# A layered attention and expert network: the initial loads in order of use, and the doubled context copied on chip

## The chip, the cores and the metric

The kernel runs as one program on one core of a Trainium2 chip. The metric is device time in microseconds (us), from one launch to its end; lower is better. The core has five engines with a queue each: PE multiplies matrices, ACT (ScalarE) and DVE (VectorE) and POOL (GpSimd) do elementwise work, SP (SyncE) issues transfers. ACT and POOL can issue transfers too. All queues are served in order: an instruction that waits holds back everything behind it on its engine.

## What is computed

Four layers, each a cross attention from the tokens to a small context followed by a feed-forward part, over 4 sequences of 512 tokens with 256 features; the context has 64 rows for each sequence. All in float32. Only the first two lines matter here:

```python
x = x + _L0_xattn_ref(_layernorm(x), ctx_1024, Wq, bq, Wkv, bkv, Wo, bo)
x = x + _L0_ffn_ref(_layernorm(x), router_w, gate_proj, up_proj, down_proj)
...

def _L0_xattn_ref(layer_input, cross_attn_input, Wq, bq, Wkv, bkv, Wo, bo):
    q = layer_input @ Wq + bq
    kv = cross_attn_input @ Wkv + bkv
    k, v = jnp.split(kv, 2, axis=-1)
    q, k, v = map(split_heads, (q, k, v))          # 16 heads of 16
    scores = jnp.einsum('bhqd,bhkd->bhqk', q, k) * D ** (-0.5)
    weights = jax.nn.softmax(scores, axis=-1)
    out = jnp.einsum('bhqk,bhkd->bhqd', weights, v)
    return merge_heads(out) @ Wo + bo
```

`_L0_ffn_ref` sends each token to the two best of eight experts.

## The kernel before

**Tiles.** The 2048 tokens lie in 16 tiles `x0` to `x15` of 128 tokens by 256 features; four tiles make one group, and one group is one sequence. The attention of layer 0 goes over the groups 0 to 3, and the work of one group is interleaved with the rest of the one before it. When a group's attention is done, its router picks experts, and POOL scatters the tokens into a DRAM buffer `xs` with eight indirect DMAs (L827). The expert blocks then read `xs` in expert order. Since blocks are padded, `xs` has to be cleared first: `clear_regions` (L298 on) writes zeros to all of it, 16 transfers of 1040 KB (L306) and one of 130 KB (L307), from a small tile `z`.

**The start.** The constructor of `Net` issues the loads that layer 0 needs and a few that come much later, in the order in which they are written:

- SP: `x0` to `x3` (L209), then `Wkv`, `Wq`, `Wo` (`load_xattn`, all on SP, through L266), then `x4` to `x15` (L221); after them `clear_regions`, which `run` calls before the attention.
- ACT: `consts` (identity, masks, index tables), the transposed context in four pieces (L215), `vecs` (bias columns), `rows` (bias rows, spread over all partitions, 771.5 KB), `router_w`, `fw`, `ctx`, `W_router`, `Wg`; then `pairs` (helper matrices of the attention), and further on `fcT` and a second `pairs` for layer 1.

`ctxT2` holds the transposed context twice, `[128, 2, 4, 2, 64]`: for each sequence its 64 context columns stand two times side by side, so that one 128-column block can be loaded into PE to make the values of both heads of a pair. It is filled by four loads, `n` over the two halves of the features and `k` over the two copies; each writes runs of 64 numbers.

**The order of work.** In the attention PE keeps the order that the code writes; on the other engines a scheduler places each instruction. For group 0 the order on PE is: keys (`ps_k`, L399, from `Wkv` and `ctxT2`), transposes of the normalized tokens (`ps_xT`, L357), queries (`ps_q`, L478), values (`ps_v`, L436), scores (`ps_cs`, L506). The other engines in between:

- DVE takes statistics of each `x` tile (L317, L318), and makes the scale and shift of a group's layer norm (`ln_rs` L322, `ln_sh` L323) after ACT's square root (`ln_sd` L320).
- ACT normalizes the four tiles (`xn`, L325), evacuates keys (`kT`, L407) and queries (`q`, L481) with their biases from `vecs`, and copies half of each transposed group (`xnT`, L288); DVE copies the other half (L290), and masks the keys by head (`kbd`, L379).
- POOL adds the output bias to the `x` tiles (L608).

**Completion semaphores.** Each transfer from SP or ACT signals its landing on one of eight semaphores, handed out in turn over both queues. A transfer waits, on the engine that issues it, until the one that used its semaphore before, as a rule eight transfers earlier, has landed.

Of the kernel before, what the change touches and what calls it, by code (L numbers as in the profile page):

```python
# [11 lines left out]
F32 = mybir.dt.float32  # L12
# [10 lines left out]
P = 128  # L23
B, S, E = 4, 512, 256
SC = 64
NH, HD = 16, 16
NT = B * S // P
GT = S // P
NC = E // P
# [14 lines left out]
V_BQ, V_BK, V_FMB, V_BQ3, V_BK3, V_LN1, V_LN2, V_END = 0, 2, 4, 5, 7, 9, 11, 13  # L44
# [4 lines left out]
R_BV, R_BO, R_FMB, R_FCB, R_BV3, R_BO3, R_RB = range(7)  # L49
# [129 lines left out]
class Banks:  # L179


    def __init__(self, pool, tag):
        self.pool, self.tag = pool, tag
# [5 lines left out]
class Net:  # L189
    def __init__(self, ctx, tc, d, out):  # L190
        self.tc, self.nc, self.d, self.out = tc, tc.nc, d, out
        nc = self.nc

        def pool(name, bufs, **kw):
            return ctx.enter_context(tc.tile_pool(name=name, bufs=bufs, **kw))

        self.const = pool("const", 1)
        self.small = pool("small", 2)
        self.routes = pool("routes", 1)
        self.xnp = pool("xn", 2)  # L200
        self.xnTp = pool("xnT", 2)
        self.dram = pool("dram", 1, space=DRAM)
        self.flip = 0

        c = self.const
        self.x = [c.tile([P, E], F32, tag=f"x{t}", name=f"x{t}") for t in range(NT)]
        xs = d["x"].rearrange("(t p) e -> p t e", p=P)
        for t in range(GT):
            nc.sync.dma_start(self.x[t], xs[:, t])  # L209
        self.cst = self.load("consts", [P, C_END], nc.scalar)  # L210

        self.ctxT2 = c.tile([P, NC, B, 2, SC], F32, tag="ctxT2", name="ctxT2")
        for n in range(NC):
            for k in range(2):
                nc.scalar.dma_start(self.ctxT2[:, n, :, k], d["ctxT"][n * P : (n + 1) * P])  # L215
        self.vecs = self.load("vecs", [P, V_END], nc.scalar)
        n_rows = d["rows"].shape[0]
        self.rows = self.load("rows", [P, n_rows], nc.scalar, d["rows"].partition_broadcast(P))
        self.W0 = self.load_xattn("Wq", "Wkv", "Wo")
        for t in range(GT, NT):  # L220
            nc.sync.dma_start(self.x[t], xs[:, t])  # L221
        self.rw0 = self.load_w("router_w", 8, nc.scalar)
        self.fw = self.load("fw", [P, P], nc.scalar)
        self.ctx = self.load("ctx", [SC, B, E], nc.scalar, d["ctx"].rearrange("b s e -> s b e"))
        self.rw1 = self.load_w("W_router", 7, nc.scalar)
        self.rw3 = self.load_w("Wg", 8, nc.scalar)

        self.ident = self.cst[:, C_ID : C_ID + P]
        self.eps = c.tile([P, 1], F32, tag="eps", name="eps")
        nc.vector.memset(self.eps, 1e-5)  # L230
        self.nfmb = c.tile([P, 1], F32, tag="nfmb", name="nfmb")
        nc.vector.tensor_scalar(self.nfmb, self.vec(V_FMB), -1.0, None, ALU.mult)

        self.xs = self.dram.tile([8 * CAP + P, R_END], F32, tag="xs", name="xs")
        self.ys = self.dram.tile([3 * STAMP, E], F32, tag="ys", name="ys")

        self.w2q = self.dram.tile([P, W2_END], F32, tag="w2q", name="w2q")
# [32 lines left out]
        rows = self.d[name].shape[0]  # L270
        return self.load(name, [P, rows // P, n], eng, self.d[name].rearrange("(c p) n -> p c n", p=P), tag, pool)

    def load_xattn(self, q, kv, o):

        eng = self.nc.sync
        return self.load_w(kv, 2 * E, eng, "Wkv"), self.load_w(q, E, eng, "Wq"), self.load_w(o, E, eng, "Wo")

    def vec(self, i):
        return self.vecs[:, i : i + 1]
# [491 lines left out]
class Routed:  # L771
# [30 lines left out]
    def add(self, g, rows, oh1, oh2):  # L802
# [5 lines left out]
        for i in range(1, GT):  # L808
            nc.vector.tensor_tensor(pm[:, i], pm[:, i - 1], mk[:, i - 1], ALU.add)
        run = self.keep(f"run{g}", [P, n])  # L810
        nc.vector.tensor_tensor(run, pm[:, GT - 1], mk[:, GT - 1], ALU.add)
        self.run = run
        ps = net.acc.tile([P, GT, n], F32, tag="acc", name="ps_rank")
# [222 lines left out]
class Layers(Net):  # L1036
# [566 lines left out]
                last = hq  # L1603
            down(NT - 1, last)

    def xattn_linear(self, Wkv, Wq, Wo, bq, bk, bv, bo, after):
        self.xattn(
            self.query_linear(Wq, bq),
            lambda pool, b: self.values_linear(pool, b, Wkv, bv),
            HD**-0.5,  # L1610
            HD,
            Wo,
            bo,
            after=after,
            keys=lambda pool: self.keys_linear(pool, Wkv, bk),
        )

    def run(self):
        nc, d = self.nc, self.d

        def banks():
            return self.banks(mm=4, tr=2, acc=2)

        W1, W3 = [], []
        moe = Routed(self, 8, 704, d["e0gu"], d["e0d"], "e0", 2 * STAMP)
        with self.room("l0w", 1) as keep:
            self.clear_regions(keep)
            self.xattn_linear(*self.W0, V_BQ, V_BK, R_BV, R_BO, after=lambda g: self.route(moe, g, self.rw0))
        with self.room("l1k", 1, side="right") as kept:
            with self.room("l0b", side="right") as pool, banks():  # L1630

                def later():
                    yield
                    yield
                    W3.extend(self.load_xattn("w_qT", "w_kvT", "w_oT"))
                    W1.append(self.load_w("fcT", E, nc.scalar, pool=kept))
                    yield from self.ctx_ready(kept, self.keys_features)
                    yield from self.l2_weights(pool)

                with self.in_order(DVE, SP):  # L1640
                    moe.blocks(pool, later())
            self.xattn(
                self.query_features, self.values_features, 1.0 / 16.0, 2 * HD, W1[0], R_FCB, before=moe
            )
        moe = self.l1_ffn()
        with banks():
            self.l2(moe)
        moe = Routed(self, 8, 512, d["e3gu"], d["e3d"], "e3", 0)
        self.xattn_linear(*W3, V_BQ3, V_BK3, R_BV3, R_BO3, after=lambda g: self.route(moe, g, self.rw3))
        with self.room("l3b", side="right") as pool, banks():  # L1650
            with self.in_order(DVE, SP):
                moe.blocks(pool)
            out = self.out.rearrange("(t p) e -> p t e", p=P)
            with self.in_order(SP, ACT, DVE, POOL):
                queues = (nc.sync, nc.scalar)
                for t in range(NT):
                    moe.load(pool, t, queues[t % 2])
                for t in range(NT):
                    moe.take(t, nc.gpsimd if t % 3 == 2 else nc.vector)
                    queues[t % 2].dma_start(out[:, t], self.x[t])  # L1660
# [21 lines left out]
```

## Time and profile before

| | |
|---|---|
| three runs | 2026.68, 2027.1, 2034.26 us; median 2027.1 |
| the profiled execution | 2033.3 us, of which 2031.5 us is its span, from the first to the last instruction |
| PE busy over the span | 1716.2 us (84%) |
| DVE, ACT, POOL busy | 974.0 us (48%), 668.2 us (33%), 420.3 us (21%) |
| PE busy from 0 to 20 us | 3.79 us |
| ACT busy from 0 to 20 us | 1.07 us |
| the 16 DMA engines from 0 to 20 us | busy 90%, 260 GB/s |
| the 16 DMA engines from 20 to 40 us | busy 106% (of a nominal rate), 316 GB/s |
| first indirect scatter into `xs` | 106.8 us |

A line of the timeline gives start, duration, engine, source line, operation, what is written from what, and a count; in brackets, how long the engine had been idle and what ended that. A "q" after the engine's name marks its queue: the instruction issues a transfer, and the engine isn't busy. The waits view adds such idle times up. The windows view gives for each stretch of time the busy time of PE, weight loads, DVE, ACT and POOL, then the granted clock of PE, the busy share of the DMA engines, and the GB/s that they moved.

### The profile page before, as it was taken

How to read it: one execution, taken by the hardware profiler on the slowest of the kernel's cores; microseconds unless marked ns; L12 is line 12 of the kernel's file. 1: busy time of each engine (PE TensorE's matmuls, PEld its weight loads, DVE VectorE, ACT ScalarE, POOL GpSimd, SP SyncE). 2: the span in 40 equal slices, each digit the busy share in tenths (PEclk: the TensorE clock that was granted, in tenths of full speed). 3: DMA queues.
4: the chain of work that ended last, by engine and by line, in shares of the span. 5: the costliest groups of instructions: out<-in, count | busy, mean ns of one | idle time of the engine just before them, and what ended most of it. 6: DMA issues, size and time to landing. Idle time of an engine off the chain costs nothing.

```text
span 2031.5 us, 25639 instructions
## 1 busy us (share of the span) xinstructions
PE 1716.2 (84%) x8740; PEld 975.9 (48%) x8740; DVE 974.0 (48%) x2778; ACT 668.2 (33%) x1254; POOL 420.3 (21%) x590
## 2 busy tenths in 40 slices
PE   4874999999959978899999878994998887599994
PEld 2443666666624533344443344443665443355662
DVE  3644344444445333445454435446899564333333
ACT  3341322222243341335344522223445333122221
POOL 1033011111150010222222322224113112311112
PEclk8986999999979987999999989996899898699997
DMA  9613878787420000000000018772000001598895
GB/s 290 182 43 127 343 292 285 283 292 279 157 93 1 17 23 0 1 1 17 6 3 20 19 34 283 263 270 88 1 0 1 12 4 40 181 313 296 305 316 170
DMA packets 111042, 271.85 MB, mean 134 GB/s; under 512 B 15488, under 2 KB 73024, under 8 KB 100800
## 3 DMA queue, kind: packets, MB, share of 16 engines
q1 hardware_dynamic: 81728, 227.35, 33.0%
q0 software_dynamic: 10176, 28.00, 3.6%
q10 hardware_dynamic: 19008, 14.86, 2.3%
q8 instruction: 70, 1.15, 0.2%
q14 instruction: 60, 0.49, 0.1%
HBM read 220.75 MB, written 49.42 MB: 133 GB/s over the span
## 4 chain that ended last, share of the span: by engine, by line
PE 63%; DVE 14%; ACT 5%; issue 3%; POOL 3%; DMA 2%; SPq 0%; ACTq 0%; DVEq 0%; POOLq 0%
PE ps_gu L938 20%; PE ps_de L980 9%; PE ps_ms L1127 4%; PE ps_mo L1165 3%; DVE mq L1132 2%; PE ps_he L967 2%; PE ps_p L592 2%; PE ps_mx L1142 2%; PE ps_f L1549 2%; POOL xs L827 2%; PE ps_bc L571 1%; PE ps_ms L1130 1%; PE ps_xT L357 1%; PE ps_xe L924 1%; PE ps_cy L577 1%
## 5 line engine op out<-in xcount | busy, mean ns | idle before, releaser
L938 PE MATMUL ps_gu<-e_wgu,e_xT 128*128 128x352 f32 (+1 forms) x1088 | 417.8, 524 | 4.7 <-DVE e_xT L930 0.8
L938 PEld LDWEIGHTS ps_gu<-e_wgu,e_xT 128*128 128x128 f32 x1088 | 197.2, 191 | 143.9 <-issue 74.0
L980 PE MATMUL ps_de<-e_wd,e_hT 128*128 128x256 f32 x932 | 232.3, 385 | 3.8 <-ACT e_hT L288 1.5
L955 DVE TENSOR_TENSOR e_h<-e_s,ps_gu 128x352 f32<-128x352 f32 (+2 forms) x155 | 83.5, 538 | 295.5 <-PE ps_gu L938 226.9
L983 POOL DMA_INDIRECT ys<-e_y,e_to x116 | 112.4, 969 | 522.4 <-ACT e_y L982 399.5
L980 PEld LDWEIGHTS ps_de<-e_wd,e_hT 128*128 128x128 f32 x932 | 172.1, 189 | 79.5 <-issue 42.3
L954 ACT ACTIVATE e_s<-ps_gu 128x352 f32<-128x352 f32 (+2 forms) x155 | 74.0, 477 | 327.6 <-PE ps_gu L938 323.5
L1132 DVE TENSOR_REDUCE mq<-ps_ms 128x2 f32<-128x256 f32 (+3 forms) x128 | 105.7, 825 | 137.8 <-PE ps_ms L1130 136.5
L982 ACT ACTIVATE e_y<-ps_de,e_wt 128x256 f32<-128x256 f32 x116 | 54.9, 473 | 259.4 <-PE ps_de L980 248.1
L1144 ACT ACTIVATE mpr<-ps_mx 128x1024 f32<-128x1024 f32 (+3 forms) x128 | 90.0, 703 | 138.7 <-PE ps_mx L1142 135.5
L1127 PE MATMUL ps_ms<-mkT,mqT 32*128 32x512 f32 (+3 forms) x512 | 111.1, 512 | 22.7 <-DVE mq L1132 21.6
L827 POOL DMA_INDIRECT xs<-xn,e_at x96 | 93.9, 978 | 135.3 <-DVE ln_rs L322 75.7
L1142 PE MATMUL ps_mx<-mqm,mkT 32*128 32x128 f32 (+3 forms) x512 | 105.6, 489 | 1.1 <-ACT mpr L1144 1.1
L1146 POOL TENSOR_SCALAR_AFFINE_SELECT mpr<-mpr 128x256 f32<-128x256 f32 x128 | 51.8, 407 | 238.6 <-ACT mpr L1144 238.5
L1165 PE MATMUL ps_mo<-mpr,va 128*32 128x128 f32 (+3 forms) x512 | 96.4, 457 | 3.0 <-POOL mpr L1146 3.0
L357 PE MATMUL ps_xT<-consts_sb,xn 128*128 128x128 f32 x256 | 52.4, 340 | 50.9 <-ACT xn L325 36.1
L967 PE MATMUL ps_he<-consts_sb,e_h 128*128 128x128 f32 x466 | 76.2, 278 | 11.9 <-DVE e_h L955 7.9
L1549 PE MATMUL ps_f<-w,xqT 128*128 128x352 f32 x256 | 84.7, 472 | 1.2 <-ACT xqT L1540 1.2
L924 PE MATMUL ps_xe<-consts_sb,e_x 128*128 128x128 f32 x232 | 51.4, 292 | 36.6 <-DMA e_x<-xs 33.6
L927 DVE COPY e_xT<-ps_xe 128x256 f32<-128x256 f32 x78 | 33.0, 423 | 98.4 <-PE ps_xe L924 98.4
L537 PE MATMUL ps_cx<-q,kbd 32*128 32x512 f32 x256 | 45.0, 803 | 39.5 <-ACT cpr L543 39.5
L1127 PEld LDWEIGHTS ps_ms<-mkT,mqT 32*128 32x128 f32 x512 | 40.8, 195 | 77.6 <-DVE mq L1132 54.4
(314 smaller groups left out, 2769.0 us busy)
## 6 DMA issues: line engine op xcount, KB each, us to landing
e_wgu<-in_e0gu SPq DMA_DIRECT2D x39, 1408.0 KB, 6.1
e_wgu<-in_e3gu SPq DMA_DIRECT2D x39, 1024.0 KB, 5.4
e_wd<-in_e0d SPq DMA_DIRECT2D x39, 768.0 KB, 5.6
e_wd<-in_e3d SPq DMA_DIRECT2D x39, 512.0 KB, 5.6
e_wgu<-in_e1gu SPq DMA_DIRECT2D x38, 512.0 KB, 4.0
xs<-z SPq DMA_DIRECT2D x16, 1040.0 KB, 15.4
e_x<-xs SPq DMA_DIRECT2D x116, 130.0 KB, 4.9
e_wd<-in_e1d SPq DMA_DIRECT2D x38, 256.0 KB, 4.1
```

What stands on the lines that cost most here:

```text
L827: r = nc.gpsimd.indirect_dma_start(out=net.xs, out_offset=bass.IndirectOffsetOnAxis(ap=at[:, k, i : i + 1], axis=0), in_=rows[:, i], in_of ...
L938: nc.tensor.matmul(ps[:, :n], xT[:, c], wgu[:, c, cols], start=(c == 0), stop=(c == NC - 1))
L955: nc.vector.tensor_tensor(h[:, k * H : (k + 1) * H], s, u, ALU.mult)
L967: self.nc.tensor.transpose(ps[:r, f - f0], h[:, f * P : f * P + r], net.ident)
L980: nc.tensor.matmul(po[:, :E], hT[:r, f], wd[:r, f], start=(f == 0), stop=(f == self.nf - 1))
L983: r = nc.gpsimd.indirect_dma_start(out=net.ys, out_offset=bass.IndirectOffsetOnAxis(ap=at, axis=0), in_=y, in_offset=None)
L1127: nc.tensor.matmul(ps[:, r, :n], st.qT[o][rows, diag], st.kT[o][rows, :n], start=True, stop=False)
L1132: nc.vector.tensor_reduce(st.q[:, i, at : at + 2, HD], ps[:, :, :n], AX.X, ALU.max, negate=True)
L1142: nc.tensor.matmul(ps[:, r, :n], st.kT[o][rows, keys], st.qm[o][rows, j * P :], start=True, stop=True)
L1144: nc.scalar.activation(pr[:, :, :n], ps[:, :, :n], AF.Exp, scale=HD**-0.5)
L1165: nc.tensor.matmul(st.po[32 * n : 32 * n + 32, j * P :], st.va[:, j, at : at + 32], pr[:, r, : S - j * P], start=(j == 0), stop=(j == GT - 1),
L1549: nc.tensor.matmul(ps[:, :H], xT[:, c], w[:, c, k * H : (k + 1) * H], start=(c == 0), stop=(c == NC - 1))
```

## The change

It changes which queue issues each initial load and in what order, and how the second copy of the context is made:

- ACT issues five loads: `consts`, the transposed context once (one load of 256 KB into a tile of the `xnT` pool, rows of 256 numbers), `Wkv`, `vecs`, and then, as before, `pairs`.
- SP issues `x0` to `x3`, `Wq`, `Wo`, the first 512 columns of `rows`, `x4` to `x7`, `router_w` between `x7` and `x8`, the other `x` tiles, the rest of `rows`, `fw`, `ctx`, `W_router`, `Wg`, and the zeros last.
- `ctxT2` is filled by four POOL copies of 128x256 from the loaded tile, first both halves of copy 0, then those of copy 1.
- `clear_regions` is called through a new argument `then`, after the keys of layer 0 are written down, instead of before the attention.

```diff
+        ctxT = self.xnTp.tile([P, NC, S], F32, tag="xnT", name="ctxT")[:, :, : B * SC]
+        nc.scalar.dma_start(ctxT, d["ctxT"].rearrange("(c p) b s -> p c (b s)", p=P))
+        Wkv, Wq, Wo = self.load_xattn("Wq", "Wkv", "Wo", (nc.scalar, nc.sync, nc.sync))
+        self.W0 = Wkv, Wq, Wo
+        self.vecs = self.load("vecs", [P, V_END], nc.scalar)
+
+        self.rows = c.tile([P, d["rows"].shape[0]], F32, tag="rows", name="rows_sb")
+
+        def rows(part):
+            nc.sync.dma_start(self.rows[:, part], d["rows"].partition_broadcast(P)[:, part])
+
+        rows(slice(0, 2 * E))
+        for t in range(GT, NT):
+            if t == 2 * GT:
+                self.rw0 = self.load_w("router_w", 8, nc.sync)
+            nc.sync.dma_start(self.x[t], xs[:, t])
+        rows(slice(2 * E, None))
+        self.fw = self.load("fw", [P, P], nc.sync)
+        self.ctx = self.load("ctx", [SC, B, E], nc.sync, d["ctx"].rearrange("b s e -> s b e"))
+        self.rw1 = self.load_w("W_router", 7, nc.sync)
+        self.rw3 = self.load_w("Wg", 8, nc.sync)
 
         self.ctxT2 = c.tile([P, NC, B, 2, SC], F32, tag="ctxT2", name="ctxT2")
-        for n in range(NC):
-            for k in range(2):
-                nc.scalar.dma_start(self.ctxT2[:, n, :, k], d["ctxT"][n * P : (n + 1) * P])
-        self.vecs = self.load("vecs", [P, V_END], nc.scalar)
-        n_rows = d["rows"].shape[0]
-        self.rows = self.load("rows", [P, n_rows], nc.scalar, d["rows"].partition_broadcast(P))
-        self.W0 = self.load_xattn("Wq", "Wkv", "Wo")
-        for t in range(GT, NT):
-            nc.sync.dma_start(self.x[t], xs[:, t])
-        self.rw0 = self.load_w("router_w", 8, nc.scalar)
-        self.fw = self.load("fw", [P, P], nc.scalar)
-        self.ctx = self.load("ctx", [SC, B, E], nc.scalar, d["ctx"].rearrange("b s e -> s b e"))
-        self.rw1 = self.load_w("W_router", 7, nc.scalar)
-        self.rw3 = self.load_w("Wg", 8, nc.scalar)
+        for k in range(2):
+            for n in range(NC):
+                nc.gpsimd.tensor_copy(
+                    self.ctxT2[:, n, :, k], ctxT[:, n].rearrange("p (b s) -> p b s", s=SC)
+                )
...
-    def load_xattn(self, q, kv, o):
-
-        eng = self.nc.sync
-        return self.load_w(kv, 2 * E, eng, "Wkv"), self.load_w(q, E, eng, "Wq"), self.load_w(o, E, eng, "Wo")
+    def load_xattn(self, q, kv, o, queues=None):
+
+        names = ((kv, 2 * E, "Wkv"), (q, E, "Wq"), (o, E, "Wo"))
+        return [
+            self.load_w(n, w, eng, tag) for (n, w, tag), eng in zip(names, queues or 3 * [self.nc.sync])
+        ]
...
+        def keys(pool):
+            yield from self.keys_linear(pool, Wkv, bk)
+            then()
...
-            self.clear_regions(keep)
-            self.xattn_linear(*self.W0, V_BQ, V_BK, R_BV, R_BO, after=lambda g: self.route(moe, g, self.rw0))
+            self.xattn_linear(
+                *self.W0, V_BQ, V_BK, R_BV, R_BO,
+                after=lambda g: self.route(moe, g, self.rw0), then=lambda: self.clear_regions(keep),
+            )
```

**The built program.** The scheduler places the instructions anew. Compared engine by engine, PE has the same instructions in the same order in both programs. On ACT, DVE and POOL the order differs only up to the first `ps_cs` of group 0; from there on it is the same, and each instruction waits for the same others. The placements at the start that the steps below use are these:

- ACT: the five loads, a table load, `ln_sd` of group 0, the load of `fcT`, the four `xn` of group 0, the first `kT`, `ln_sd` of group 1, the second load of `pairs`, the second `kT`, the copy of `xnT`, the four `xn` of group 1, the first `q`, `ln_sd` of group 2, one `xn`, the second `q`. The table load in front of `kT` is gone.
- DVE: statistics of `x0` to `x3`, `nfmb` (from `vecs`), statistics of `x4`, `ln_rs` of group 0, statistics of `x5`, `ln_sh` of group 0, statistics of `x6` to `x11`, two `kbd`, `ln_rs` and `ln_sh` of group 1, the copy of `xnT`, two `kbd`.
- POOL: the memsets, `none`, the four copies of the context, then the additions of the bias.
- Semaphores: the loads of `vecs`, `pairs` and `fcT` wait for the landings of `x0`, the context and the first part of `rows`; `x4` and `x5` for those of `x2` and `x3`; `x9` for that of the first `pairs`; the second `pairs` for that of `x9`.

More of the change, by code (lines that the diff above doesn't have):

```diff
@@ L1604, in l2, with xattn_linear @@
             down(NT - 1, last)
-    def xattn_linear(self, Wkv, Wq, Wo, bq, bk, bv, bo, after):
+    def xattn_linear(self, Wkv, Wq, Wo, bq, bk, bv, bo, after, then=lambda: None):
+        def keys(pool):
+            yield from self.keys_linear(pool, Wkv, bk)
+            then()
         self.xattn(
@@ L1614, in xattn_linear @@
             after=after,
-            keys=lambda pool: self.keys_linear(pool, Wkv, bk),
+            keys=keys,
         )
```

## The prediction

> **What bounds the kernel now.** I read the page first: PE is busy 84% of the span, but slice by slice it starts with 4 tenths, while the DMA line starts with 9. The start is a stage of its own. Then the timeline of each engine over the first 40 us. ACT's:
>
> ```profile
> 1.25 4.00 ACTq L215 DMA_DIRECT2D ctxT<-in_ctxT  x4
> ...
> 13.55 0.67 ACTq L266 DMA_DIRECT2D ctx_sb<-in_ctx  x1
> ...
> 18.49 0.35 ACTq L266 DMA_DIRECT2D pairs_sb<-in_pairs  x1
> 18.93 1.28 ACT L407 ACT_TABLE_LOAD   x1 [18.93 <-DMA x<-in_x]
> 20.23 0.47 ACT L407 ACTIVATE kT<-ps_k,vecs_sb 128x256 f32<-128x256 f32 x1
> ...
> 21.08 1.28 ACT L320 ACT_TABLE_LOAD   x1
> 22.38 0.49 ACT L320 ACTIVATE ln_sd<-ln_mv,eps 128x4 f32<-128x4 f32 x2
> 23.16 2.57 ACT L325 ACTIVATE xn<-x,ln_sh,ln_rs 128x256 f32<-128x256 f32 x5 [0.29 <-DVE ln_sh L323]
> ```
>
> ACT computes nothing before 18.93 us. The "DMA" behind it is no operand: ACT stands behind its own 13 issues, several of them held until an older transfer lands. Next PE and DVE:
>
> ```profile
> 8.51 3.79 PE L399 MATMUL ps_k<-ctxT,Wkv_sb 128*128 128x256 f32 x8 [8.51 <-DMA Wkv_sb<-in_Wkv]
> 23.81 2.81 PE L357 MATMUL ps_xT<-consts_sb,xn 128*128 128x128 f32 x8 [11.51 <-ACT xn L325]
> 26.44 5.63 PE L478 MATMUL ps_q<-xnT,Wq_sb 128*128 128x512 f32 x8
> ...
> 32.87 1.17 PE L506 MATMUL ps_cs<-kbd,q 32*128 32x128 f32 x32
> ...
> 6.89 0.18 DVE L318 BATCH_NORM_AGGREGATE ln_mv<-ln_st 128x2 f32<-128x6 f32 x1
> ...
> 13.56 0.43 DVE L317 BATCH_NORM_STATS2 ln_st<-x 128x6 f32<-128x256 f32 x1 [2.85 <-DMA x<-in_x]
> ```
>
> Group 0's statistics are ready at 7.07 us and the keys are multiplied by 12.3, yet PE waits 11.51 us for `xn`. That hole is the prize. The waits view between 0 and 60 us says the same, and the windows view shows what else is there:
>
> ```profile
> PE ps_xT L357 <- ACT xn L325: 11.5, 1, 11.5
> ```
>
> ```profile
> 0.00:10.00 10.00, 1.49 (x4) 1.04 (x5) 2.88 (x12) 0.00 (x0) 1.44 (x11) 1.00 0.88 251
> 10.00:20.00 10.00, 2.30 (x6) 1.32 (x4) 2.88 (x11) 1.07 (x1) 0.00 (x0) 1.00 0.92 269
> ...
> 80.00:90.00 10.00, 9.13 (x58) 4.79 (x58) 2.90 (x2) 4.81 (x6) 0.72 (x1) 0.75 0.18 51
> ```
>
> Last, SP's timeline with the zeros, and the scatters into `xs` (name, count, shortest/median/longest in ns, first and last start):
>
> ```profile
> 18.91 54.95 SPq L306 DMA_DIRECT2D xs<-z  x16
> 73.91 3.55 SPq L307 DMA_DIRECT2D xs<-z  x1
> ```
>
> ```profile
> L827 POOL DMA_INDIRECT xs<-xn,e_at x32: 965/971/1178, 106.8 to 191.7; - x32
> ```
>
> The DMA engines are nearly full from the first microsecond: 2.51 MB in the first 10 us, 2.69 MB in the next. So data, not ACT, is the next limit. The last zeros land at 84.4 (73.91 plus the 10.5 us to landing of the page's issue table); the first scatter into `xs` starts at 106.8. PE fills up only after 50 us.
>
> **What the Trainium skill says.** "DMA: Bandwidth & Descriptors", section "Anatomy of one DMA", says that DMA engines don't wait on semaphores: the issuing sequencer waits before it dispatches. ACT's empty 18.93 us agree. The same page, "Issuing engines are not separate DMA queues", says that spreading transfers over engines saves only issue time. Here that is exactly what is for sale: 13 issues ahead of ACT's first arithmetic become five; the bytes cost what they cost (0.88 and 0.92 busy above). "TensorE: Matmul & The Clock Gate", Part 1, gives a half clock after an idle window and the full one after about 3.4 us of activity. The trace agrees in kind: weight loads of `ps_q` are 0.85 us apart until 30.0 and 0.43 after. Where in that the new start falls I can't know.
>
> **The change part by part.** Times are those of the profiled execution.
>
> *Removed from ACT.* Eight net issues, and one of two table loads of 1.28 us (the built order has the square root first, and the keys then need no other table). ACT is left with waits for `x0` (landed before DVE's first statistics at 3.76) and for the context, then a table load: `ln_sd` of group 0 can run at about 7.5 us, when the statistics are there.
>
> *What is late next.* In the built order DVE takes the statistics of `x4` and `x5` before `ln_sh` of group 0, and ACT's `xn` needs `ln_sh`. So `xn` waits for `x5`. When does it land? Check the meter on before: up to `x4` the queues carried `consts` 0.27, `x0`–`x3` 0.52, context 0.52, `Wkv` 0.52, `Wq` and `Wo` 0.52, `rows` 0.79, `x4` 0.13, together 3.27 MB; the windows give 2.51 + 3.5 x 0.269 = 3.45 MB at 13.5 us, where `x4` was let in. Good to half a microsecond. After, up to `x5`: 0.27 + 0.79 (`x0`–`x5`) + 0.26 (context once) + 0.52 + 0.52 + 0.26 (first `rows`) = 2.62 MB, plus between none and all of `pairs` (0.56), which goes along on ACT's queue: 10.4 to 12.5 us. The queues share, so I take 12.3. Then statistics 0.43, `ln_sh` 0.18 and a gap: `xn` at 13.1, the first transpose 0.65 later (23.16 to 23.81 now) at 13.75. `ps_k` is out of the way: even with `Wkv` at 9.5 instead of 8.5, its 3.8 us end at 13.3.
>
> *ACT up to the queries.* Four `xn` at 0.51 to 15.2; `kT` 0.47, `ln_sd` 0.3 to 15.95. Then the second `pairs` is issued, and waits for `x9`, with `kT` and `xnT` behind it and PE behind them. `x9` adds 0.52 MB of `x` and a part of `fcT` (0.52) to 3.18 MB: 3.70 to 4.22 MB, 14.4 to 16.4 us; but it is issued only when the first `pairs` is down (about 12.5), and an `x` takes 4.1 us (median) from issue to landing: I take 16.3. Issue 0.35, `kT` 0.47, `xnT` 0.59: `ps_q` at 17.8 instead of 26.44, 8.6 us earlier. The other half of `xnT` is DVE's and stands behind the statistics of `x11`: 0.26 MB later, 17.0, plus 0.43, two `kbd` 0.70, four small ones 0.7, copy 0.69: 19.5, just when PE has done its first two cold passes of 0.85. No cover is left there: each microsecond that `x11` is late costs one.
>
> *From `ps_q` to `ps_cs`* it takes 6.43 us now. ACT puts `ln_sd` of group 2 and one `xn` between the two `q`, and that `xn` waits for a DVE step in between: I add 0.3. `ps_cs` starts at 24.5 instead of 32.87: 8.3 us earlier. From there all engines have the same order and waits as before.
>
> *Added to POOL.* Four one-input copies of 128x256. Nearest rows: 407 ns (L1146, one input) and 724 ns (L608, two inputs). The skill's "GPSIMD Engine Reference", section 4.1, puts one-input work near line rate; I take 0.45. Two must be done for `ps_k`: context at 6 (issued at about 1.25, as now, and 4 to 5.5 us to landing by the issue table), so 6.9 to 7.5, under the cover of `Wkv` at 9 or later. Without that cover they would cost 1.5 us at most. The other two are needed at `ps_v`, 10 us later. The bias additions behind them need `xn` at 13 or later.
>
> *Moved on SP.* Six more issues at about 0.4 us stand before the zeros; most hide in waits for landings. The zeros start near 19 as now, and with 0.26 MB less to carry end near 85. The first scatter comes at 106.8 − 8.3 = 98.5: 13 us of slack. Nothing else is behind the zeros on SP until the expert tables, over 100 us later. `router_w`, `fw`, `ctx`, `W_router`, `Wg`, the rest of `rows`: needed at 88 us or later, free.
>
> *Sum.* 2033.3 − 8.3 = 2025.0 us for an execution like the profiled one; that lies 6.2 above the median of the runs shown, so for the median 2027.1 − 8.3 = 2018.8 us.
>
> **Rivals.**
>
> *Everything comes sooner.* `x5` lands at 10.4, `x9` at 14.4; `xn` then has only `ps_k` (13.3) in its way, `ps_q` starts near 16.3, and PE, busier from 9.5 on, has its full clock for the last four passes of `ps_q` (4 x 0.42 = 1.7 us). 26.44 − 16.3 + 1.7 = 11.8: 2015.3. For it: less data in front, and the context in rows four times as long. Against it: three landings in a row must all be early.
>
> *Loads late.* Eight semaphores couple the queues, and POOL, ACT and DVE each hold a line behind one landing. With `x9` or `x11` at 20.5 instead of 16.5, the gain is 4 us: 2023. For it: ACT's 544 KB and 512 KB now go in between the `x` tiles.
>
> *The zeros decide.* If the zeros, now last, land after the scatter at 98.5, POOL waits for them, and then routing and the experts. From 98.5 each microsecond costs one, from 106.8 the kernel is slower than before. The fill takes 65.5 us now (18.91 to 84.4); at two thirds of its rate it would take 98 and end at 117.5: 2027.1 + 10.7 = 2038. Against it: the same transfers on the same queue, beside less traffic than now.
>
> *No effect.* If the early lead were absorbed before the experts, 2027. Against it: no wait in the windows from 32 to 107 us ends with a load.
>
> **How the numbers follow.** 0.5% of 2027.1 is 10.1 us, about what a measurement of this kernel can tell from no change; three runs alone span 7.6. Forecast 2018.8 (2017 to 2021 for itself): 0.50. Sooner, 2015.3: 0.26. Late, 2023: 0.15. Zeros, 2038: 0.05. No effect: 0.04. Under 2017.0 lie the sooner case and a seventh of the forecast: faster 0.33. Slower 0.06 by the zeros and a little noise; 0.61 within. From 2013.5 to 2024 leaves out the zeros, no effect, and the ends of sooner and late, together near 0.2.
>
> **What would show it.** Right: ACT's first table load near 6 to 7 us; `xn` released by `ln_sh` near 13; the second `pairs` issued near 16.3; `ps_q` near 17.8; `ps_cs` near 24.5; the first scatter near 98.5, released by DVE; POOL's copies 0.4 to 0.7 us. Wrong if `ps_q` starts after 22, if `ps_k` waits for POOL, if a zero transfer releases the scatter, or if the lead at `ps_cs` isn't the lead at the scatter.

## The result, and the profile after

The change makes the kernel faster by about 8 us. Twelve runs of the changed kernel have a median of 2027.87 us (2021.48 to 2032.27), twelve of the kernel before, the three of the prediction among them, 2033.84 us (2026.68 to 2048.35). The medians differ by 6.0 us and the means by 8.2; the ratio estimated from all these runs is 0.9962, 95% interval 0.9945 to 0.9979: 7.7 us, between 4.3 and 11.2. Two later comparisons, on two chips, gave 0.9957 (0.9940 to 0.9973) and 0.9961 (0.9948 to 0.9974). Gains in time below are worked out from such ratios.

The forecast gain was 8.3 us, and lies well inside that interval. The forecast time missed: 2018.8 us, range 2013.5 to 2024.0, against 2027.87. The profiled execution took 2026.92 us (span 2025.2), where the sum made on the profiled execution before had given 2025.0.

ACT's timeline of the changed kernel over the first 40 us (start, us, engine, line, operation; in brackets the idle time before it and what ended it):

```profile
1.24 0.46 ACTq L213 DMA_DIRECT2D ctxT<-in_ctxT  x1
1.73 0.49 ACTq L279 DMA_DIRECT2D Wkv_sb<-in_Wkv  x1
...
5.21 0.35 ACTq L279 DMA_DIRECT2D pairs_sb<-in_pairs  x1
5.58 1.28 ACT L335 ACT_TABLE_LOAD   x1 [5.58 <-DMA ctxT<-in_ctxT]
8.16 0.30 ACT L335 ACTIVATE ln_sd<-ln_mv,eps 128x4 f32<-128x4 f32 x1 [1.29 <-DVE ln_mv L333]
11.96 0.39 ACTq L279 DMA_DIRECT2D fcT_sb<-in_fcT  x1
14.40 2.08 ACT L340 ACTIVATE xn<-x,ln_sh,ln_rs 128x256 f32<-128x256 f32 x4 [5.94 <-DVE ln_sh L338]
...
16.54 0.34 ACTq L279 DMA_DIRECT2D pairs_sb<-in_pairs  x1
...
17.29 0.58 ACT L303 COPY xnT<-ps_xT 128x512 f32<-128x512 f32 x1
```

ACT is free at 5.58 us, where it stood until 18.93. `ln_sd` no longer waits for ACT but for DVE. The 5.94 us ahead of `xn` are a new wait, one engine further on: `ln_sh`, which DVE computes only after the statistics of `x4` and `x5`. DVE's timeline shows what holds it:

```profile
13.28 0.43 DVE L332 BATCH_NORM_STATS2 ln_st<-x 128x6 f32<-128x256 f32 x1 [4.26 <-DMA x<-in_x]
...
14.22 0.14 DVE L338 SCALAR_TENSOR_TENSOR ln_sh<-ln_mv,ln_rs 128x4 f32<-128x4 f32 x1
```

A transfer of `x`, and so the load queue, is the limit now. PE's timeline of the changed kernel:

```profile
8.27 3.75 PE L414 MATMUL ps_k<-ctxT,Wkv_sb 128*128 128x256 f32 x8 [8.27 <-DMA Wkv_sb<-in_Wkv]
15.05 2.81 PE L372 MATMUL ps_xT<-consts_sb,xn 128*128 128x128 f32 x8 [3.03 <-ACT xn L340]
17.92 5.17 PE L493 MATMUL ps_q<-xnT,Wq_sb 128*128 128x512 f32 x8
...
23.88 1.17 PE L521 MATMUL ps_cs<-kbd,q 32*128 32x128 f32 x32
```

PE's hole shrank from 11.51 to 3.03 us, and `ps_cs` starts 9.0 us earlier (32.87 to 23.88). The windows view of the changed kernel (busy time of PE, its weight loads, DVE, ACT and POOL, then PE's granted clock, DMA share and GB/s):

```profile
0.00:10.00 10.00, 1.73 (x4) 1.49 (x5) 2.87 (x13) 1.58 (x2) 2.97 (x15) 1.00 0.81 252
10.00:20.00 10.00, 6.85 (x16) 3.50 (x16) 6.00 (x25) 4.62 (x11) 3.25 (x5) 1.00 0.91 291
```

The DMA engines carry about what they carried; PE does 6.85 us of work in the second 10 us instead of 2.30. SP's zeros, and the scatters into `xs`:

```profile
20.55 49.99 SPq L321 DMA_DIRECT2D xs<-z  x16
70.59 4.31 SPq L322 DMA_DIRECT2D xs<-z  x1
```

```profile
L842 POOL DMA_INDIRECT xs<-xn,e_at x96: 957/972/1183, 97.5 to 1752.1; - x96
```

The zeros land at 81.6 us, 16 us ahead of the first scatter (97.5, was 106.8). They decide nothing.

How far does the lead carry? For each instruction found in both traces I took its start after minus its start before, and of fifteen neighbours the median, in us, against the place in the trace of before:

| place, us | 34 | 160 | 520 | 640 | 760 | 1100 | 1160 | 1380 | 1430 | 2030 |
|---|---|---|---|---|---|---|---|---|---|---|
| after − before | −9.0 | −9.4 | −9.5 | −11.3 | −12.9 | −12.8 | −8.9 | −9.4 | −6.2 | −6.3 |

In this pair of traces the lead is made in the first 33 us and kept to 520. Then it moves in steps. At the same work near 1142 us before and 1129 us after, the windows of before, and then of after, say why:

```profile
1142.00:1146.00 4.00, 4.00 (x38) 2.73 (x38) 1.62 (x3) 2.53 (x3) 0.81 (x2) 1.00 0.00 0
1146.00:1150.00 4.00, 4.00 (x19) 1.06 (x14) 3.69 (x20) 2.09 (x2) 0.41 (x1) 0.57 0.02 4
```

```profile
1129.00:1133.00 4.00, 3.79 (x21) 1.63 (x20) 1.05 (x2) 1.64 (x2) 0.41 (x1) 0.50 0.00 0
1133.00:1137.00 4.00, 4.00 (x22) 3.53 (x26) 1.24 (x3) 1.92 (x3) 0.41 (x1) 0.50 0.00 0
1137.00:1141.00 4.00, 4.00 (x22) 0.82 (x14) 3.69 (x19) 2.09 (x2) 0.41 (x1) 0.56 0.00 0
```

PE is busy throughout in both, but its clock (third number from the end) is 0.50 for two windows more in the changed kernel: 38 matmuls in 4 us before, 21 and 22 in 4 us after. Near 610 us it is the other way round; the windows of before, and then of after:

```profile
609.00:614.00 5.00, 5.00 (x14) 1.81 (x7) 3.36 (x1) 2.96 (x7) 3.91 (x6) 0.50 0.00 0
```

```profile
600.00:605.00 5.00, 4.85 (x72) 3.19 (x72) 4.18 (x4) 4.62 (x10) 3.91 (x6) 1.00 0.00 0
```

Whether these steps belong to the change is a question for the experiments.

### The profile page after: what moved, and what is told of

The parts are those of the page before. It is cut to its first block, busy times and chain, and to the rows that moved or that the text cites. A ratio compares the mean times of both kernels' runs of the same rounds, so it can differ in the third digit from the quotient of the medians.

```text
span 2025.2 us, 25644 instructions
## 1 busy us (share of the span) xinstructions
PE 1719.9 (85%) x8740; PEld 980.1 (48%) x8740; DVE 974.2 (48%) x2778; ACT 667.5 (33%) x1253; POOL 423.5 (21%) x594
## 4 chain that ended last, share of the span: by engine, by line
PE 64%; DVE 14%; ACT 5%; issue 3%; POOL 3%; DMA 2%; SPq 0%; ACTq 0%; DVEq 0%; POOLq 0%
PE ps_gu L953 20%; PE ps_de L995 9%; PE ps_ms L1142 4%; PE ps_mo L1180 3%; DVE mq L1147 2%; PE ps_he L982 2%; PE ps_mx L1157 2%; PE ps_f L1564 2%; PE ps_p L607 2%; POOL xs L842 2%; PE ps_bc L586 1%; PE ps_ms L1145 1%; PE ps_xe L939 1%; PE ps_xT L372 1%; PE ps_cy L592 1%
```

## The experiments

My theory: ACT stood behind its own issues, and taking eight of them away makes a gain at the first `ps_cs` that goes through to the end; the base of the forecast was wrong, not the gain. Rivals: fewer bytes bring it; the later steps belong to the change.

| kernel | first `ps_cs` at | ratio to before, 95% interval | its median, and that of before on the same chip |
|---|---|---|---|
| before | 32.87, again 32.73 | 1 | |
| after | 23.88 | 0.9962 (0.9945–0.9979) | 2027.87, 2033.84 |
| after, again | 25.51 | 0.9957 (0.9940–0.9973) | 2034.00, 2041.69 |
| after, third | 26.04 | 0.9961 (0.9948–0.9974) | 2031.55, 2040.17 |
| e1, late loads back on ACT | 29.19 | 0.9987 (0.9976–0.9998) | 2032.72, 2034.47 |
| e2, context alone | 27.28 | 0.9966 (0.9947–0.9985) | 2029.11, 2034.47 |
| e3, all but the context | 27.45 | 0.9978 (0.9964–0.9992) | 2030.78, 2034.47 |
| e9, e3 with `Wkv` first | 26.55 | 0.9973 (0.9959–0.9987) | 2033.99, 2040.17 |
| e4, `x4`–`x7` first | 23.93 | 0.9946 (0.9927–0.9965) | 2024.05, 2034.47 |
| e10, e4 again | 24.01 | 0.9946 (0.9929–0.9963) | 2030.17, 2040.17 |
| e8, e4 with PE kept busy | 23.35 | 0.9962 (0.9951–0.9973) | 2034.40, 2041.69 |
| e5, the zeros twice | 24.12 | one run | 2061.69, 2041.69 |

### e1: the late loads back on ACT

```diff
...
-        rows(slice(0, 2 * E))
+        n_rows = d["rows"].shape[0]
+        self.rows = self.load("rows", [P, n_rows], nc.scalar, d["rows"].partition_broadcast(P))
         for t in range(GT, NT):
-            if t == 2 * GT:
-                self.rw0 = self.load_w("router_w", 8, nc.sync)
             nc.sync.dma_start(self.x[t], xs[:, t])
...
-        self.fw = self.load("fw", [P, P], nc.sync)
+        self.rw0 = self.load_w("router_w", 8, nc.scalar)
+        self.fw = self.load("fw", [P, P], nc.scalar)
```

`ctx`, `W_router` and `Wg` go back in the same way.

> This is the changed kernel with the six late loads (rows whole, router_w, fw, ctx, W_router, Wg) put back on ACT, between vecs and pairs; the context is still loaded once and copied by GpSimd, the zeros are still last on SP. Theory 'ACT stood behind its issues': ACT's first arithmetic (ln_sd of group 0) goes back from 8.2 us to 15 us or later, ps_q starts at 23 to 26 us instead of 17.9, the first ps_cs at 30 to 32 us instead of 23.9, and the total returns to within 3 us of the kernel before (about 2032). Rival 'fewer bytes and the on-chip copy bring the gain': ps_cs stays at 24 to 26 us and the total keeps 6 us or more of the gain.

ACT's timeline of this kernel:

```profile
16.10 0.35 ACTq L273 DMA_DIRECT2D pairs_sb<-in_pairs  x1
16.48 1.28 ACT L416 ACT_TABLE_LOAD   x1 [16.48 <-DMA ctx_sb<-in_ctx]
...
19.92 0.49 ACT L329 ACTIVATE ln_sd<-ln_mv,eps 128x4 f32<-128x4 f32 x2
```

`ln_sd` is back at 19.92 us, `ps_q` at 23.99, and of the 9.0 us 3.7 are left at `ps_cs`; the time is 2.6 us under before (0.4 to 4.9). ACT comes free 2.45 us earlier than in before (16.48 against 18.93), and `ps_q` starts 2.45 us earlier (23.99 against 26.44): with the same order behind it, what ACT's queue gains arrives in full. `ps_cs` came 0.8 us earlier than expected, because `ps_q` took 4.42 us instead of 5.17 to 5.63. The single context load and the on-chip copy were still there: the place of the issues is worth 5.3 us at `ps_cs`, with the second table load, which stands in this order again, among them.

### e2: the context alone

```diff
-        for n in range(NC):
-            for k in range(2):
-                nc.scalar.dma_start(self.ctxT2[:, n, :, k], d["ctxT"][n * P : (n + 1) * P])
+        ctxT = self.xnTp.tile([P, NC, S], F32, tag="xnT", name="ctxT")[:, :, : B * SC]
+        nc.scalar.dma_start(ctxT, d["ctxT"].rearrange("(c p) b s -> p c (b s)", p=P))
+        for k in range(2):
+            for n in range(NC):
+                nc.gpsimd.tensor_copy(
+                    self.ctxT2[:, n, :, k], ctxT[:, n].rearrange("p (b s) -> p b s", s=SC)
+                )
```

> This is the kernel before with one part of the change alone: the context is loaded once on ACT and doubled by four GpSimd copies; all other issues stay where they were. ACT has ten issues before its arithmetic instead of thirteen. Theory 'ACT stood behind its issues': most of the hold stays, ps_cs starts at 29 to 33 us instead of 32.9, and the total lies 0 to 4 us under the kernel before. Rival 'fewer bytes': 0.26 MB less at 0.27 MB per us is 1 us, and if the smaller descriptors of the doubled context cost more than their bytes, up to 6 us: ps_cs at 26 to 28 us.

My band for my own theory failed: 27.28 lies in the rival's. ACT's timeline tells which mechanism it was:

```profile
14.94 0.35 ACTq L270 DMA_DIRECT2D pairs_sb<-in_pairs  x1
15.32 1.28 ACT L324 ACT_TABLE_LOAD   x1 [15.32 <-DMA x<-in_x]
16.62 0.30 ACT L324 ACTIVATE ln_sd<-ln_mv,eps 128x4 f32<-128x4 f32 x1
...
17.36 0.59 ACT L329 ACTIVATE xn<-x,ln_sh,ln_rs 128x256 f32<-128x256 f32 x1
```

ACT's queue is through 3.61 us earlier (15.32 against 18.93), though it still issues ten transfers: in before the four context issues alone hold it from 1.25 to 5.25. The other 2.2 us to `xn` (17.36 against 23.16) come from the order: the scheduler set `ln_sd` ahead of the keys here, and one table load and the wait behind the keys are gone. Fewer bytes did not bring the data sooner (`x4` at 13.41 and `x5` at 14.60 us, against 13.54 and 13.91; `ps_k` starts at 8.46 against 8.51). So it is ACT's queue after all, and I had counted issues where I should have counted the time they stand. Why the end of the queue moves by just 3.6 us isn't taken apart: the last hold, of `pairs` for the landing of `ctx`, ends at 14.9 instead of 18.5, and `ctx` itself was issued at 6.27 instead of 13.55, since with three transfers fewer each issue waits for another landing. From 34 us to the end the lead of this trace stays between about 5.5 and 6.3 us, and is 5.8 at the end: in this trace what is won at `ps_cs` goes through one to one.

### e3 and e9: all but the context, and `Wkv` ahead of it

e3 loads the doubled context by four transfers on ACT as before (the lines that e2 removes), in the place of `ctxT` and its copies. e9 moves them:

```diff
-        self.ctxT2 = c.tile([P, NC, B, 2, SC], F32, tag="ctxT2", name="ctxT2")
-        for n in range(NC):
-            for k in range(2):
-                nc.scalar.dma_start(self.ctxT2[:, n, :, k], d["ctxT"][n * P : (n + 1) * P])
         Wkv, Wq, Wo = self.load_xattn("Wq", "Wkv", "Wo", (nc.scalar, nc.sync, nc.sync))
         self.W0 = Wkv, Wq, Wo
+        self.ctxT2 = c.tile([P, NC, B, 2, SC], F32, tag="ctxT2", name="ctxT2")
+        for n in range(NC):
+            for k in range(2):
+                nc.scalar.dma_start(self.ctxT2[:, n, :, k], d["ctxT"][n * P : (n + 1) * P])
```

> This is the changed kernel without its GpSimd copies: the doubled context is loaded by four transfers on ACT as before, everything else as changed. ACT issues eight before its arithmetic instead of five. Theory 'ACT stood behind its issues': three more issues of about 0.4 to 1 us and the holds behind them put ln_sd of group 0 at 9 to 11 us; since xn waits for x5 at about 14 us anyway, ps_cs moves from 23.9 to 24.5 to 26 us and the total is 0.5 to 2 us worse than the changed kernel. Rival 'the on-chip copy is what pays': ps_cs returns to 28 us or later, 4 us or more of the gain lost.

> This is the kernel of the third experiment (changed kernel, doubled context by four transfers on ACT) with Wkv issued ahead of the four instead of behind them. Theory 'the four context transfers cost by what stands behind their 4.2 us of issue, above all Wkv': ps_k starts at 9 to 11 us instead of 13.3, and the first ps_cs at 24 to 26 us instead of 27.5, close to the changed kernel's 23.9 to 25.5; time within 3 us of the changed kernel. Rival 'the doubled context in 256-byte pieces costs as such, wherever it stands': ps_cs stays at 27 us or later.

Timelines of e3, ACT, then PE, then DVE:

```profile
1.25 4.17 ACTq L215 DMA_DIRECT2D ctxT<-in_ctxT  x4
5.63 0.45 ACTq L274 DMA_DIRECT2D Wkv_sb<-in_Wkv  x1
...
12.20 1.28 ACT L330 ACT_TABLE_LOAD   x1 [12.20 <-DMA Wkv_sb<-in_Wkv]
13.49 0.30 ACT L330 ACTIVATE ln_sd<-ln_mv,eps 128x4 f32<-128x4 f32 x1
...
17.08 0.47 ACT L417 ACTIVATE kT<-ps_k,vecs_sb 128x256 f32<-128x256 f32 x1 [0.66 <-PE ps_k L409]
17.46 2.56 ACT L335 ACTIVATE xn<-x,ln_sh,ln_rs 128x256 f32<-128x256 f32 x5
```

```profile
13.29 3.75 PE L409 MATMUL ps_k<-ctxT,Wkv_sb 128*128 128x256 f32 x8 [13.29 <-DMA router_w_sb<-in_router_w]
```

```profile
16.47 0.43 DVE L327 BATCH_NORM_STATS2 ln_st<-x 128x6 f32<-128x256 f32 x1 [0.74 <-DMA x<-in_x]
...
17.21 0.15 DVE L333 SCALAR_TENSOR_TENSOR ln_sh<-ln_mv,ln_rs 128x4 f32<-128x4 f32 x1
```

Timelines of e9, PE and then ACT (where the four issues stand from 1.73 to 7.71 us, and the table load comes at 10.52):

```profile
8.01 1.19 PE L409 MATMUL ps_k<-ctxT,Wkv_sb 128*128 128x256 f32 x2 [8.01 <-DMA ctxT<-in_ctxT]
11.36 2.93 PE L409 MATMUL ps_k<-ctxT,Wkv_sb 128*128 128x256 f32 x6 [2.15 <-DMA ctxT<-in_ctxT]
```

```profile
16.86 2.57 ACT L335 ACTIVATE xn<-x,ln_sh,ln_rs 128x256 f32<-128x256 f32 x5 [1.88 <-DVE ln_sh L333]
```

e3 lost 3.6 us of the lead at `ps_cs`, where my theory allowed at most 2, and `ln_sd` came at 13.49 instead of 9 to 11. `Wkv` is issued 3.9 us later than in the changed kernel, and the keys start 5.0 us later. e9 gives back 0.9 of the 3.6: `ps_k` starts at 8.01, but the last six of its eight matmuls wait for the later context transfers, and ACT is still held to 10.52. Neither band of e9 was hit (26.55, between 26 and 27).

The four issues, each of 0.55 to 0.67 us, take 4 to 6 us of ACT's time with their waits, but this isn't what `xn` waits for in the two kernels: `ln_sd` is done at 13.8 in e3 and 12.1 in e9, and `xn` starts at 17.46 and 16.86. Both were scheduled anew, and the order is not that of the changed kernel. There DVE takes only `x4` and `x5` ahead of `ln_sh`, and ACT no `kT` ahead of `xn`. Here DVE takes the statistics of `x4` to `x9` first (in e9 the four `kbd` as well), and ACT both `kT`. So in e3 `xn` stands behind the keys (the second `kT` at 17.08) and, hardly less, behind the landing of `x8` (16.45 us); in e9, where the keys are early, the place of `ln_sh` on DVE remains. The 3.6 us are the price of four issues together with the order made around them; how much is ACT's stand alone isn't shown.

The two parts together: context alone 5.6, the rest alone 5.4, both 9.0. They overlap by 2 us. That both shorten the same stand of ACT would give such an overlap; with three different orders in play it is not shown.

### e4 and e10: `x4` to `x7` first

```diff
-        Wkv, Wq, Wo = self.load_xattn("Wq", "Wkv", "Wo", (nc.scalar, nc.sync, nc.sync))
-        self.W0 = Wkv, Wq, Wo
+        Wkv = self.load_w("Wkv", 2 * E, nc.scalar, "Wkv")
+        Wq = self.load_w("Wq", E, nc.sync, "Wq")
...
-        rows(slice(0, 2 * E))
         for t in range(GT, NT):
             if t == 2 * GT:
+                rows(slice(0, 2 * E))
+                self.W0 = Wkv, Wq, self.load_w("Wo", E, nc.sync, "Wo")
                 self.rw0 = self.load_w("router_w", 8, nc.sync)
```

> This is the changed kernel with x4 to x7 issued ahead of the first part of rows and of Wo on SP. Theory 'x5 is the next limit' (DVE takes the statistics of x4 and x5 ahead of ln_sh of group 0, and x5 landed at 13.6 us): x5 lands near 11 us, xn starts at 11.5 to 12.5 us instead of 14.4, the first ps_xT at 12.2 to 13 us instead of 15.05; the second pairs is then held by x9 at about 16.5 as now, so ps_q moves from 17.9 by less than that, to 16.5 to 17.5, and the total gains 0.5 to 1.5 us on the changed kernel. Rival 'the DMA engines share what they carry, order on a queue does little': x5 still lands at 13 us or later and ps_q stays within 0.3 us of 17.9.

> This is the changed kernel with x4 to x7 issued first, unaltered, beside the changed kernel on the same chip. Theory 'landings at the start vary and what follows hides the rest': first ps_cs at 23.5 to 25 us, time within 2 us of the changed kernel. Rival 'x first is the better order': time 2 to 4 us under the changed kernel, as the ratios of the two earlier calls (0.9946 against 0.9957 and 0.9962) would allow.

ACT's timeline of e4:

```profile
13.33 2.07 ACT L341 ACTIVATE xn<-x,ln_sh,ln_rs 128x256 f32<-128x256 f32 x4 [4.23 <-DVE ln_sh L339]
...
16.59 0.33 ACTq L280 DMA_DIRECT2D pairs_sb<-in_pairs  x1
```

`x5` landed at 10.85 us instead of 13.58, as expected, but `xn` moved only from 14.40 to 13.33: in this kernel's order DVE takes `x4` to `x7` ahead of `ln_sh`. And that did not help `ps_q` (17.98 against 17.92), for the second `pairs` still waits for `x9`, which landed at 16.57. The expected 0.4 to 1.4 us at `ps_q` did not come; the second wait that the prediction named took the place of the first. In e10, the same kernel again, `ps_q` was at 17.27 and `ps_cs` at 24.01. Against the changed kernel on the same chip e10 is 1.4 us lower by the medians (2030.17 and 2031.55) and 3 us by the ratios, and the intervals overlap. It is the lowest of the versions, but a difference from the changed kernel isn't shown.

### e5: the zeros twice

```diff
-        for n in range(rows.shape[0]):
+        for n in 2 * list(range(rows.shape[0])):
             nc.sync.dma_start(rows[n], z[:, None].to_broadcast([P, 8, R_END]))
```

> This is the changed kernel with each of the sixteen large fills of xs issued twice in a row of thirty-two; the second pass writes the same zeros again. Theory 'the zeros have slack and then decide': one fill takes 3.9 us now, so the last lands at 81.6 + 16 x 3.9 = 144 us; the first scatter, at 97 us in the changed kernel, moves to 140 to 148 us, and the time rises by 20 to 47 us (part of the move may be made up while GpSimd catches up). Rival 'no scatter waits for the fill': the first scatter stays within 3 us of 97 and the time rises by less than 5 us.

POOL's timeline between 90 and 200 us, of e5 and then of the changed kernel on the same chip (e6):

```profile
148.91 1.18 POOL L842 DMA_INDIRECT xs<-xn,e_at  x1 [55.28 <-issue]
...
161.46 1.04 POOL L842 DMA_INDIRECT xs<-xn,e_at  x1 [0.53 <-POOL xn L813]
```

```profile
99.52 1.18 POOL L842 DMA_INDIRECT xs<-xn,e_at  x1 [4.49 <-DVE ln_mv L333]
...
131.85 1.04 POOL L842 DMA_INDIRECT xs<-xn,e_at  x1 [20.35 <-DVE ln_rs L337]
```

The first scatter comes at 148.9 instead of 99.5, 49.4 us later, and the one run took 2061.69 us against a median of 2034.00: 28 us (26 against the profiled run of e6). "Issue" in the bracket means that the view names no releaser; that it is the fill follows from the edit, which doubles nothing else, and from SP, which issues its last fill from 136.5 to 140.7 us (in the changed kernel the last one lands 11 us after it starts to be issued). So the rival is real: scatters do wait for the zeros. But its price was too high. "From 98.5 each microsecond costs one" fails: of 49.4 us only 29.6 reach the next group's scatter (161.46 against 131.85), because POOL had stood idle 20 us ahead of it.

### e6, e7 and e11: both kernels unaltered, again

> This is the changed kernel unaltered, profiled and timed once more. Theory 'the start is fixed, later differences are the PE clock falling differently': first ps_cs again within 0.4 us of 23.9, while the lead over the kernel before differs by 1 to 4 us from the first trace somewhere after 500 us. The ratio to the kernel before is again 0.9945 to 0.998, and the median of the kernel before is 2033 to 2038, not 2027. Rival 'the later changes of the lead belong to the change': the lead goes through the same steps, near 610, 710, 1148 and 1415 us, as in the first trace.

> This is the kernel before unaltered, profiled once more. First ps_cs within 0.4 us of 32.9. Theory 'the later differences are the PE clock falling differently': against its first trace it shifts by 1 to 4 us in steps after 500 us, with nothing changed. Rival: its marks stay within 0.5 us of the first trace all the way.

> This is the changed kernel unaltered, profiled and timed for the third time. Theory 'gain of the start, and landings that vary': first ps_cs between 23.5 and 25.8 us (23.9 and 25.5 before), ratio to the kernel before 0.9945 to 0.998, whatever the median of the kernel before is on this chip. Rival 'the gain depends on the chip as the time does': ratio outside that.

The kernel before, against its own first trace, and the two second traces against each other (made on the same chip), by the measure used above:

| place, us | 34 | 160 | 520 | 640 | 760 | 1100 | 1160 | 1380 | 1430 | 2030 |
|---|---|---|---|---|---|---|---|---|---|---|
| before again − before | −0.1 | 2.1 | 4.3 | 1.2 | −0.4 | 0.0 | 4.3 | 8.0 | 8.7 | 10.3 |
| after again − before again | −7.2 | −9.2 | −9.9 | −8.4 | −7.0 | −7.0 | −7.1 | −6.7 | −6.5 | −7.6 |

Two executions of the same program differ by 10.3 us at the end, in steps as large as the change. (Which chip the first trace is from isn't known, so part of the 10.3 can be the chip's; but 48 runs of this kernel on one chip also lie between 2029.12 and 2047.53.) In the second pair the lead takes other steps than in the first: it shrinks at 640, where it grew, and doesn't move at 1160 or 1430. So the steps after 520 us are not the change's. Nor is it fixed to a microsecond before that: in the second pair it grows from 7.2 to 9.9 us between 34 and 520, and the kernel before moved by 2.1 to 4.3 against itself there.

The expectation of the start failed, and so did that of 2033 to 2038 us for the median of before in e6 (2041.69). The changed kernel's `ps_cs` stood at 25.51 and 26.04 in these traces, 1.6 and 2.2 us later than in the first. PE's timeline of e6 and of e11:

```profile
18.51 2.08 PE L493 MATMUL ps_q<-xnT,Wq_sb 128*128 128x512 f32 x2 [0.89 <-ACT xnT L303]
20.83 3.89 PE L493 MATMUL ps_q<-xnT,Wq_sb 128*128 128x512 f32 x6 [0.25 <-DVE xnT L305]
```

```profile
16.97 2.08 PE L493 MATMUL ps_q<-xnT,Wq_sb 128*128 128x512 f32 x2
19.55 5.49 PE L493 MATMUL ps_q<-xnT,Wq_sb 128*128 128x512 f32 x6 [0.50 <-DVE xnT L305]
```

In e6 the loads come later: DVE meets `x9` at 17.12 us (16.54 in the first trace), and its half of `xnT`, behind the statistics, is what PE waits for. In e11 the loads are early, but `ps_q` runs at half rate (the granted clock from 17 to 25 us is 0.50): its last six records take 5.49 us instead of 3.89. Over the three traces the gain at `ps_cs`, against the mean 32.8 of the two of before, is 8.9, 7.3 and 6.8: mean 7.7.

The times of before settle the other question. Nine further runs beside the first result have a median of 2037.74 us; on three other chips, 48 runs have 2034.47, 26 have 2041.69 and 41 have 2040.17. The lowest of these 124 runs together is 2029.12 us. Two of the three runs that the prediction had, 2026.68 and 2027.10, lie below all of them.

### e8: PE kept busy ahead of the queries

This is e4 with eight more matmuls, whose results nobody reads:

```diff
+        def warm(n):
+            ps = self.mm.tile([P, 512], F32, name="ps_w")
+            for _ in range(n):
+                self.nc.tensor.matmul(ps, self.ident, self.cst[:, :512], start=True, stop=True)
+
         def keys(pool):
+            if bq == V_BQ:
+                warm(5)
             yield from self.keys_linear(pool, Wkv, bk)
+            if bq == V_BQ:
+                warm(3)
             then()
```

> This is the kernel with x4 to x7 first, and eight extra matmuls of 128x512 on constants, whose results nobody reads: five before ps_k, three after it. Theory 'the start now pays for a PE that runs its first passes at half rate': ps_k takes 1.9 to 2.5 us instead of 3.75, ps_q 3.4 to 4 us instead of 5.2, the first ps_cs comes at 22 to 22.8 us instead of 23.9, and the time falls by 1 to 2 us more. Rival 'loads set the pace there': ps_q starts where it did (18 us), its second half waits for xnT, and ps_cs stays at 23.5 us or later.

PE's timeline:

```profile
10.43 1.89 PE L415 MATMUL ps_k<-ctxT,Wkv_sb 128*128 128x256 f32 x8
...
17.41 1.12 PE L494 MATMUL ps_q<-xnT,Wq_sb 128*128 128x512 f32 x2 [0.78 <-ACT xnT L304]
19.71 2.84 PE L494 MATMUL ps_q<-xnT,Wq_sb 128*128 128x512 f32 x6 [1.18 <-DVE xnT L306]
```

PE ran its passes faster: `ps_k` took 1.89 us instead of 3.75, and the passes of `ps_q` 3.96 instead of 5.16. But PE then waited 1.18 us for DVE's `xnT`, and `ps_cs` came at 23.35, 0.6 us earlier than in e4. The time is that of the changed kernel (2034.40 and 2034.00). The rival holds: at `ps_q` the loads and DVE's queue behind them set the pace (DVE waits 3.02 us for `x8`, and from there to `xnT` it works without a pause), and a quicker PE waits.

## Why the prediction was right or wrong

| step of the prediction | said | measured, first trace |
|---|---|---|
| ACT's first table load | 6 to 7 | 5.58 |
| `ln_sd` of group 0 | 7.5 | 8.16 |
| `x5` lands | 12.3 | 13.58 |
| `xn` | 13.1 | 14.40 |
| first `ps_xT` | 13.75 | 15.05 |
| `ps_k` ends | 13.3 at the latest | 12.0 |
| second `pairs` issued | 16.3 | 16.54 |
| `ps_q` | 17.8 | 17.92 |
| DVE's half of `xnT` ready | 19.5 | 19.4 |
| first `ps_cs` | 24.5 | 23.88 |
| a context copy on POOL | 0.45 | 0.40 (four, overlapping, in 1.43) |
| zeros: start, landed | 19, 85 | 20.55, 81.6 |
| first scatter into `xs` | 98.5 | 97.5 |
| gain (all runs) | 8.3 | 7.7 (4.3 to 11.2) |

**The failed step is the last line of the sum**: "that lies 6.2 above the median of the runs shown, so for the median 2027.1 − 8.3 = 2018.8". The sum of the parts gave 2025.0 for an execution like the profiled one, and the changed kernel's profiled execution took 2026.92. Taking off another 6.2 us assumed that the three runs' median was what the kernel before takes, and the profiled execution a slow one. The runs show the reverse: in 124 further runs the medians are 2034 to 2042, and the profiled 2033.3 was the better base. The median of before in the comparison less the forecast gain is 2033.84 − 8.3 = 2025.5. What made those three runs low, another chip or chance, stays open; nothing recorded with them tells it. That 8.3 came so near to 7.7 is in part luck: the interval is 6.9 us wide, and at `ps_cs` the three traces gained 8.9, 7.3 and 6.8.

**The range failed with it.** It was built from unknown costs in the first 30 us (2017 to 2021 for the likeliest case, cases from 2013.5 to 2024), and left out what the other 2000 us do from one execution to the next. The prediction had the sign of it in hand: its three runs span 7.6 us, and the profiled execution lay 6.2 away from their median. The changed kernel's own twelve runs span 10.8, the two traces of before 10.6.

**The mechanism was right.** ACT behind its issues (e1, e2), data as the next limit (DVE's wait above), `x5` and `x9` as the two landings that hold ACT (e4: with `x5` early, `x9` holds alone), PE then short of DVE's half of `xnT` (e6, e8). *Sizes that were off:* `x5` was 1.3 us late, and covered, since the second `pairs` waited for `x9` in any case. The meter on before was good to 0.7 us, not to half a microsecond (3.45 less 3.27 MB at 0.269 MB per us), and 0.26 MB after 16.3 is 17.3, not 17.0 (`x11` landed at 17.2). The half-rate passes of `ps_q` ended sooner in the first trace, which made `ps_cs` 0.6 us earlier than said; in e11 they didn't, and it was 1.5 later. "The queues share, so I take 12.3" was near the late end of the bytes' range, and still too early: by 13.58 us 3.6 MB had moved, not the 2.6 to 3.2 counted up to `x5`, since the transfers issued after it share the engines with it.

**What the sum didn't price** is what each part is worth by itself. "Eight net issues" was right as a total; three of them, the context's, are worth 5.6 of the 9.0 us when they go first (e2) and 3.6 when they go last (e3), with the order around them changed both times.

**The rivals.** *Everything comes sooner*: not in the first trace, where `x5` and `x9` landed after the forecast. In e11 the loads were early and `ps_q` started at 16.97, not far from this rival's 16.3; but it counted on PE's full clock for the last passes, and there PE was back at half rate, so that `ps_cs` came last of the three. *Loads late*: the mechanism is there (e6, 1.6 us), a size of 4 us not. *The zeros decide*: not here, 16 us of slack; real when the fill is doubled (e5), at 0.5 to 0.6 us for each, not 1. *No effect*: excluded, the interval ends at 0.9979.

## What to carry to other kernels

Take a gain that was worked out on a profiled execution off that execution's own time, and before moving to the median of a few runs ask whether the gap between the two isn't just the spread: three runs that span 7.6 us can't carry a correction of 6.2 and a range of ±5. When an engine stands behind its own DMA issues, price the time it stands, holds between the issues included, and not the number of issues: here four issues of 0.6 us took 4 to 6. After such a stand is removed, look for the landing that the next instruction in the order waits for; moving one load forward (`x5`) did not bring `ps_q` forward in e4, while the next (`x9`) held the same queue. And where a scheduler places the instructions of each version anew, compare the orders before naming the cause of a difference: in e3 and e9 the order had moved as well as the loads.

## What the runs showed of the hardware that had not been expected

- The same kernel has medians of 2034.47, 2041.69 and 2040.17 us on three chips, 0.35% apart, while the ratio of the two kernels is 0.9957 and 0.9961 on the latter two, and 0.9962 in the first comparison. Here the ratio carried from chip to chip, and the time didn't.
- PE's clock falls to 0.50 for stretches of 4 us and more amid busy work, and where it does so differs between two executions of one kernel (from 1140 to 1150 us its mean is 0.83 in the first trace of before and 0.50 in the second, which does the same work there up to 4.3 us later). "TensorE: Matmul & The Clock Gate", Part 1, of the Trainium skill says that activity is judged in a window of some 3.4 us that runs freely, not from the kernel's start, so that the same kernel shows different counts of slow matmuls in different runs. The traces agree: same orders, other places. The table of the two states there gives one idle window or more as what brings the half clock back; near 1127 us in the changed kernel no window of that length is idle (PE is busy 4.15 us of the 5 from 1125), so that part the trace doesn't show. The steps here are up to 4 us each.
- A 1.00 in the clock column at the start isn't a measured full clock: up to the first change of the clock that a trace records, the view gives 1.00. That first change is one to the full clock, at 30.4 us in before, 20.9 in the changed kernel, 23.0 in e6 and 7.8 in e8. So `ps_k` took 3.75 us in the changed kernel and 1.89 in e8. In e11 the full clock comes at 11.7, goes at 15.1 and is back at 25.3, in step with `ps_q` at half rate. The stretches between these first changes last 3.4, 6.8, 10.2, 13.7, 20.5, 27.3 and 30.7 us, whole multiples of 3.4.
